# A gated-experts layer in fp32 on one core: the down projection as 2x4x4 block products in 26 multiplications (was 28), worked inside the unit that makes its inputs

## The chip, the core and the metric

The kernel runs on one core of one Trainium2 chip. The metric is the device time in microseconds of a whole execution, median of several runs. Beside the runs, one profiled execution is shown; its trace holds every instruction of every engine. The engines are named as the profile does: PE is TensorE (PEld its weight load), DVE is VectorE, ACT is ScalarE, POOL is GpSimd, SP is the engine whose queue issues most DMAs.

## The reference

The input x is (8, 512, 256): eight blocks of 512 tokens with 256 features. Its gates are (8, 8) and the shared gate is (8). There are eight experts and one shared expert, each with Wg and Wu (256 x 1024) and Wd (1024 x 256). All is fp32.

```python
g = jnp.einsum('bsd,edf->ebsf', h, Wg)
u = jnp.einsum('bsd,edf->ebsf', h, Wu)
expert_outs = jnp.einsum('ebsf,efd->ebsd', jax.nn.silu(g) * u, Wd)
expert_output = jnp.einsum('be,ebsd->bsd', gating_probs, expert_outs)
shared = jnp.einsum('bsf,fd->bsd', jax.nn.silu(h @ Sg) * (h @ Su), Sd)
out = x + (1.0 - sg) * expert_output + sg * shared
```

## The kernel before

**Tiling.** The batch is worked in two halves of four blocks (NH = 2, NI = 4). Features of an expert are taken in groups of 4 x 128 (GRP = 2). A *unit* is one half, one expert (nine with the shared one) and one group: 2 x 9 x 2 = 36 units, each numbered u.n. In a unit, a 4 x 4 grid of results h[i, j] (feature tile i of 128, batch block j of 512 tokens) is made for gate (m = 0) and up (m = 1), and then multiplied down to two tiles of 128 output features for each block.

**Gate and up products.** The grid with inner size 2 (256 features of x in two halves) isn't computed plainly with 32 products for each m, but with 26, by a scheme of shared terms. Each i has a number CI (0, 1, -1, 2). A *hub* makes the four diagonal results: P products (raw weights, first half of x), Q products accumulated on the same PSUM bank. The six pairs (i, j) in PAIRS then take three products each: an R1 product of a difference of weights U with a difference of inputs V, and two R products. `gate_up` (L549 on) is a generator: each of its 52 steps issues one product (a G). A hub has 16 of them, each of the six *blocks* of a pair 6. The bank that a pair's R1 accumulates on is seeded by ScalarE from f (`seed`, L417), which is the difference of two P results; f is made by `make_f` (L383), from a bank by VectorE (three pairs) or from SBUF copies by GpSimd (the other three). After R1, VectorE writes D minus the bank to a second bank (L437); after the last R product, it adds D (L450). `finish` (L353) then takes silu on ScalarE for m = 0, and for m = 1 VectorE multiplies silu, gate coefficient and bank to h (L363). GpSimd makes all weight forms: `make_at`, `w_difference` (U), `w_sums` (W, L282 and L276/L279).

**Down products.** `down` (L467) does the 4 x 4 grid of h as a 2 x 2 arrangement (I for features, J for blocks) of 2 x 2 products in seven multiplications (x = 1 to 7): 2 x 2 x 7 = 28 products a unit. The sums of h that they need (`T_sums`, L455) and of Wd (`load_d`, s, L339 to L342) are made on GpSimd. Each of the 14 sums over all units lives in SBUF (acc); it is copied into a PSUM bank by ScalarE (L482), two products are accumulated on it (L491), and ScalarE copies it back (L506). Two banks, po0 and po1, alternate for that. The 28 products of a unit are issued one by one (a D) among the G of the *next* unit.

**Order.** PE and POOL run in the order that the program writes (`manual_schedule`, HAND); in the first unit ACT too. For DVE and ACT a planner sets the order at build time. The strings HUB and BLOCKS say how G and D alternate. At the unit that closes a half, the results are combined, transposed back (`turn_back`, L531), added to x and stored; the next half's x is loaded and transposed meanwhile (`turn_x`, L138), and its forms of x are made (`make_forms`, L168) and kept in DRAM scratch, from where later units load v and b. The last unit's 28 D follow all G.

Of the kernel before, what the change touches and what calls it, by code (L numbers as in the profile page):

```python
# [16 lines left out]
def kernel(  # L17
# [30 lines left out]

    nc = tc.nc
# [10 lines left out]
    FBANK = 3  # L60

    PLAIN = ()
# [8 lines left out]
    ppool = ctx.enter_context(tc.tile_pool(name="p", bufs=16))  # L71
    hapool = ctx.enter_context(tc.tile_pool(name="ha", bufs=10))
    hbpool = ctx.enter_context(tc.tile_pool(name="hb", bufs=13))
    tpool = ctx.enter_context(tc.tile_pool(name="t", bufs=6))
# [3 lines left out]
    dpool = ctx.enter_context(tc.tile_pool(name="d", bufs=3))  # L78
# [44 lines left out]
    po_next = [0]  # L123

    def new_po(name, turns=False):

        k = po_next[0]
        if not turns:
            po_next[0] = 1 - k
        return ps_o.tile([P, S], F32, tag=f"po{k}", name=name), k  # L130
# [38 lines left out]
    def make_forms(h, p):  # L169

        i, j = PAIRS[p]
        d = CI[i] - CI[j]
        v, b0, b1 = (
            zpool.tile([P, S], F32, tag="z", name=f"f{k}{h}_{p}") for k in range(3)
        )
        ve.tensor_sub(v, xhub[h, i][:, 0], xhub[h, j][:, 0])
        if d != 1.0:
            nc.scalar.mul(v, v, 1.0 / d)
        ve.tensor_add(b0, v, xhub[h, j][:, 1])
        gp.tensor_tensor(b1, v, xhub[h, i][:, 1], ALU.add)  # L180
        made.append((h, p, (v, b0, b1)))
# [8 lines left out]
    def x_difference(u, p):  # L190

        i, j = PAIRS[p]
        if plain(u, p):
            return
        v = vpool.tile([P, S], F32, tag="v", name=f"v{u.name}_{p}")
        if (u.h, p) not in scratch:
            d = CI[i] - CI[j]
            ve.tensor_sub(v, xhub[u.h, i][:, 0], xhub[u.h, j][:, 0])
            if d != 1.0:
                nc.scalar.mul(v, v, 1.0 / d)  # L200
# [4 lines left out]
    def x_sums(u, p):  # L205
# [3 lines left out]
        if plain(u, p):  # L209
            return  # L210
# [37 lines left out]
    for h in range(NH):  # L248
        for e in range(NE):
            for g in range(GRP):  # L250
# [7 lines left out]
                u.wd, u.T, u.sg, u.store = {}, {}, {}, []  # L258
# [13 lines left out]
    def scaled_sum(out_, s, a, b, sub):  # L272

        if s in (1.0, -1.0):
            if s == 1.0:
                gp.tensor_tensor(out_, a, b, ALU.subtract if sub else ALU.add)  # L276
            else:
                assert not sub
                gp.tensor_tensor(out_, b, a, ALU.subtract)  # L279
        else:  # L280
            nc.scalar.mul(out_, a, s)  # L281
            gp.tensor_tensor(out_, out_, b, ALU.subtract if sub else ALU.add)  # L282

    def make_at(u, i):
# [5 lines left out]
        if CI[i] == 2.0 and (u.opens or units[u.n - 1].opens):  # L290
            gp.tensor_tensor(t, raw[:, :, 0], raw[:, :, 1], ALU.add)
            gp.tensor_tensor(t, t, raw[:, :, 0], ALU.add)
            u.at[i] = t
            return
        scaled_sum(t, CI[i], raw[:, :, 0], raw[:, :, 1], False)
        u.at[i] = t

    def plain(u, p):
        return u.n == 0 and p in PLAIN

    def w_difference(u, p):
        i, j = PAIRS[p]
        if plain(u, p):
            return
# [4 lines left out]
    def w_sums(u, p):  # L309
        i, j = PAIRS[p]  # L310
        d = CI[i] - CI[j]
        if plain(u, p):

            u.W[p] = []
            for r, (k, c) in enumerate(((i, CI[j]), (j, CI[i]))):
                a, A = u.raw[k][:, :, 0], u.raw[k][:, :, 1]
                if c != 0.0:
                    t = upool.tile([P, 2, P], F32, tag="u", name=f"m{u.name}_{p}_{r}")
                    scaled_sum(t, c, a, A, False)
                    A = t  # L320
                u.W[p].append(A)
            return
        W = bpool.tile([P, 2, 2, P], F32, tag="wb", name=f"wb{u.name}_{p}")
        scaled_sum(W[:, 0], -d, u.raw[i][:, :, 0], u.U[p], False)
        scaled_sum(W[:, 1], d, u.raw[j][:, :, 0], u.U[p], True)
        u.W[p] = W

    def load_d(u, pairs):
        for I in pairs:
            t = dpool.tile([P, 2, D], F32, tag="wd", name=f"wd{u.name}_{I}")  # L330
            r0 = (NI * u.g + 2 * I) * P
            nc.sync.dma_start(
                t,
                weights(u.e)[2][r0 : r0 + 2 * P].rearrange("(c p) d -> p c d", p=P),
            )
            s = dpool.tile([P, 4, P], F32, tag="sd", name=f"sd{u.name}_{I}")
            a11, a21 = t[:, 0, 0:P], t[:, 0, P : 2 * P]
            a12, a22 = t[:, 1, 0:P], t[:, 1, P : 2 * P]
            gp.tensor_tensor(s[:, 0], a21, a22, ALU.add)  # L339
            gp.tensor_tensor(s[:, 1], s[:, 0], a11, ALU.subtract)  # L340
            gp.tensor_tensor(s[:, 2], a11, a21, ALU.subtract)
            gp.tensor_tensor(s[:, 3], a12, s[:, 1], ALU.subtract)  # L342
            u.wd[I] = {
                1: a11, 2: a12, 3: s[:, 3], 4: a22, 5: s[:, 0], 6: s[:, 1], 7: s[:, 2]
            }

    def new_bank(u, m, name, spare=False):

        if spare and u.n == 0:
            turned[m] = False  # L350
            return ps_o.tile([P, S], F32, tag=f"po{m}", name=f"{name}{m}_{u.name}")
        return ps_g.tile([P, S], F32, tag=f"g{m}", name=f"{name}{m}_{u.name}")

    def finish(u, m, i, j, bank):
# [4 lines left out]
        else:  # L359
            b = NI * u.h + j  # L360
            pool, tag = (hapool, "ha") if j < 2 else (hbpool, "hb")
            t = pool.tile([P, S], F32, tag=tag, name=f"h{i}{j}_{u.name}")
# [6 lines left out]
    def P_step(u, i, m):  # L369
        bank = new_bank(u, m, f"c{i}{i}", i == 3)  # L370
# [4 lines left out]
        t = ppool.tile([P, S], F32, tag="p", name=f"P{i}{m}_{u.name}")  # L375
        nc.scalar.copy(t, bank)  # L376
        u.Ps[i, m] = t
        for p in range(FBANK):
            if max(PAIRS[p]) == i:
                make_f(u, p, m, bank)  # L380

    def make_f(u, p, m, bank=None):

        if plain(u, p) or (p, m) in u.f:
            return
        i, j = PAIRS[p]
        f = zpool.tile([P, S], F32, tag="z", name=f"f{i}{j}{m}_{u.name}")
        if bank is None:
            gp.tensor_tensor(f, u.Ps[j, m], u.Ps[i, m], ALU.subtract)  # L389
        elif i > j:  # L390
            ve.tensor_sub(f, u.Ps[j, m], bank)  # L391
        else:
            ve.tensor_sub(f, bank, u.Ps[i, m])
        u.f[p, m] = f

    def Q_step(u, i, m):
# [6 lines left out]
        t = ppool.tile([P, S], F32, tag="p", name=f"D{i}{m}_{u.name}")  # L403
        nc.scalar.copy(t, bank)  # L404
        u.Ds[i, m] = t

    def plain_step(u, p, m, r, k):
        i, j = PAIRS[p] if r == 0 else PAIRS[p][::-1]
        if k == 0:
            u.bank[i, j, m] = new_bank(u, m, f"c{i}{j}")  # L410
        nc.tensor.matmul(
            u.bank[i, j, m], u.W[p][r][:, m] if k else u.raw[i][:, m, 0],
            xhub[u.h, j][:, k], start=k == 0, stop=k == 1,
        )
        if k:
            finish(u, m, i, j, u.bank[i, j, m])

    def seed(u, p):

        i, j = PAIRS[p]  # L420
        for m in range(2 if not plain(u, p) else 0):
            u.bank[j, i, m] = new_bank(u, m, f"c{j}{i}", p % 2 == 1)
            nc.scalar.copy(u.bank[j, i, m], u.f[p, m])  # L423

    def R1_step(u, p, m):
        i, j = PAIRS[p]
        if plain(u, p):
            for k in range(2):
                plain_step(u, p, m, 0, k)
            return  # L430
# [8 lines left out]
    def R_step(u, p, m, r):  # L439
        if plain(u, p):  # L440
            plain_step(u, p, m, 1, r)
            return
# [11 lines left out]
    def T_sums(u, J, x):  # L454

        for I in range(2):
            h = {(r, c): u.h_.get((2 * I + r, 2 * J + c)) for r in range(2) for c in range(2)}
            a, b = {
                5: (h[0, 1], h[0, 0]), 6: (h[1, 1], u.T.get((J, I, 5))),
                7: (h[1, 1], h[0, 1]), 4: (h[1, 0], u.T.get((J, I, 6))),  # L460
            }[x]
            t = tpool.tile([P, S], F32, tag="t", name=f"T{x}_{I}{J}_{u.name}")
            eng = ve if I == 1 and u.n + 1 == len(units) else gp
            eng.tensor_tensor(t, a, b, ALU.subtract)  # L464
            u.T[J, I, x] = t

    def down(u, acc, last):  # L467


        for J in range(2):  # L470
            for n, x in enumerate((1, 5, 2, 6, 3, 7, 4) if last else (1, 5, 3, 2, 6, 7, 4)):
                ahead = (6, None, 7, 4)[n] if n < 4 else None
                if ahead:
                    T_sums(u, J, ahead)
                if n == 4 and J == 0:
                    T_sums(u, 1, 5)
                po, k = new_po(f"po{x}_{J}_{u.name}")
                opens = (J, x) not in acc
                seeded = not opens and not turned[k]
                turned[k] = False  # L480
                if seeded:
                    nc.scalar.copy(po, acc[J, x])  # L482
                for I in range(2):
                    b = {
                        1: u.h_[2 * I, 2 * J], 2: u.h_[2 * I + 1, 2 * J],
                        3: u.h_[2 * I + 1, 2 * J + 1],
                    }.get(x)
                    if b is None:
                        b = u.T[J, I, x]
                    first = not seeded and I == 0  # L490
                    nc.tensor.matmul(  # L491
# [60 lines left out]
    def gate_up(u, nxt):  # L552
# [34 lines left out]
        for p in range(len(PAIRS)):  # L587
# [12 lines left out]
            if p == 5:  # L600
                store_made()
# [147 lines left out]
```

## Time and profile before

| | before |
|---|---|
| median of three runs | 2524.13 us (2523.95 to 2524.53) |
| profiled execution, its own time | 2520.21 us |
| its span, first to last instruction | 2518.4 us |
| granted TensorE clock | 0.999 |
| HBM read, written | 227.84 MB, 13.63 MB |
| median time to landing of b, v, wd | 3.5, 2.6, 2.7 us |

The span lies within the execution's own time. A group of the profile gives the line, the engine and operation, output and inputs by their names in the program, the shapes and the count; then the busy time, the mean of one in ns, and how long the engine was idle just before instructions of this group, with what ended the idle time. Each 128x512 product leaves two records on PE, whose ends are modelled, so that records overlap; rates are best read from the starts. The rows by stage give, for a stretch of the span, its length and the busy time of each engine in it, with the number of instructions.

### The profile page before, as it was taken

To read this page: it belongs to the slowest core of one execution; us is meant where nothing else is said; L and a number is where in the kernel's file an instruction comes from. 1 tells how busy PE (TensorE), PEld (TensorE's weight loads), DVE (VectorE), ACT (ScalarE), POOL (GpSimd) and SP (SyncE) were. 2 spreads that over 40 slices of the span, in tenths; PEclk is the share of its full clock that TensorE was granted. 3 is DMA by queue.
4 is the path that set the end of the run, shared out by engine and by line. 5 is a ranking of instruction groups with operands and counts; after the bars stand their busy time and mean duration, and the time that the engine had idled before them with its cause. 6 is when DMAs were issued, how large, how long until landed. Compare 5 with 4: busy or idle time off the path is not lost.

```text
span 2518.4 us, 21862 instructions
## 1 busy us (share of the span) xinstructions
PE 2497.1 (99%) x5896; PEld 1107.9 (44%) x5896; DVE 1213.0 (48%) x1744; ACT 1493.3 (59%) x2798; POOL 1662.4 (66%) x1868
## 2 busy tenths in 40 slices
PE   8999999999999999999999999999999999999999
PEld 3444444444444444444444444444444444444444
DVE  6544444444444444444674444444444444444445
ACT  4566666656556666666444666666665656666663
POOL 6766666676666666666786666666676666666664
PEclk9999999999999999999999999999999999999999
DMA  4323233333323323322434322232233332332222
GB/s 168 100 84 91 89 89 89 94 101 96 97 89 99 88 84 92 88 91 87 162 129 123 99 89 80 88 96 88 87 98 97 100 97 88 100 88 80 89 84 83
DMA packets 181034, 242.92 MB, mean 96 GB/s; under 512 B 13872, under 2 KB 122416, under 8 KB 180912
## 3 DMA queue, kind: packets, MB, share of 16 engines
q1 hardware_dynamic: 180624, 241.49, 31.7%
q8 instruction: 48, 0.79, 0.1%
q14 instruction: 74, 0.61, 0.1%
q10 hardware_dynamic: 288, 0.04, 0.0%
HBM read 227.84 MB, written 13.63 MB: 96 GB/s over the span
## 4 chain that ended last, share of the span: by engine, by line
PE 98%; DMA 1%; DVE 0%; ACT 0%; issue 0%; SPq 0%; DVEq 0%; ACTq 0%
PE po L491 34%; PE c L445 29%; PE c L432 15%; PE c L398 10%; PE c L372 10%; DMA xin<-in_x_dram 1%; PE ptx L134 0%; PE pto L134 0%; DVE h L363 0%; ACT c L423 0%; DVE acc L508 0%; ACT to L543 0%; ACT wb L281 0%; DVE x L160 0%; DVE acc L512 0%
## 5 line engine op out<-in xcount | busy, mean ns | idle before, releaser
L445 PE MATMUL c<-b,wb 128*128 128x512 f32 x1728 | 815.4, 593 | 0.0
L363 DVE SCALAR_TENSOR_TENSOR h<-sg,coef,c 128x512 f32<-128x512 f32 x576 | 430.3, 747 | 609.5 <-PE c L445 374.7
L506 ACT COPY acc<-po 128x512 f32<-128x512 f32 x477 | 278.3, 583 | 447.0 <-PE po L491 442.4
L445 PEld LDWEIGHTS c<-b,wb 128*128 128x128 f32 x1728 | 328.2, 190 | 409.7 <-issue 383.7
L357 ACT ACTIVATE sg<-c 128x512 f32<-128x512 f32 x576 | 343.7, 597 | 216.1 <-PE c L445 118.6
L464 POOL TENSOR_TENSOR T<-h,h 128x512 f32<-128x512 f32 x284 | 357.3, 1274 | 145.7 <-PE po L491 98.0
L437 DVE TENSOR_TENSOR c<-D,c 128x512 f32<-128x512 f32 x432 | 299.7, 694 | 307.9 <-ACT sg L357 283.4
L282 POOL TENSOR_TENSOR wb<-wb,u 128x256 f32<-128x256 f32 x216 | 154.8, 738 | 443.5 <-ACT wb L281 443.5
L432 PE MATMUL c<-v,u 128*128 128x512 f32 x864 | 436.2, 593 | 8.2 <-ACT c L423 8.2
L491 PE MATMUL po<-T,sd 128*128 128x512 f32 x864 | 435.4, 593 | 1.9 <-ACT to L543 1.5
L450 DVE TENSOR_TENSOR c<-c,D 128x512 f32<-128x512 f32 x432 | 300.2, 695 | 213.4 <-PE c L445 212.8
L464 POOL TENSOR_TENSOR T<-h,T 128x512 f32<-128x512 f32 x284 | 356.7, 1278 | 13.1 <-PE po L491 13.1
L423 ACT COPY c<-f 128x512 f32<-128x512 f32 x432 | 255.7, 592 | 150.1 <-DVE h L363 114.7
L491 PE MATMUL po<-h,wd 128*128 128x512 f32 x576 | 293.5, 592 | 0.0
L482 ACT COPY po<-acc 128x512 f32<-128x512 f32 x465 | 276.3, 594 | 22.8 <-DVE acc L508 13.0
L372 PE MATMUL c<-x,w 128*128 128x512 f32 x576 | 276.3, 592 | 0.3 <-DVE x L158 0.3
L389 POOL TENSOR_TENSOR f<-P,P 128x512 f32<-128x512 f32 x216 | 272.6, 1277 | 0.0
L432 PEld LDWEIGHTS c<-v,u 128*128 128x128 f32 x864 | 164.0, 190 | 217.2 <-issue 180.5
L491 PEld LDWEIGHTS po<-T,sd 128*128 128x128 f32 x864 | 163.5, 190 | 206.4 <-issue 202.9
L398 PE MATMUL c<-x,at 128*128 128x512 f32 x432 | 203.0, 592 | 0.5 <-DVE f L391 0.5
L404 ACT COPY D<-c 128x512 f32<-128x512 f32 x288 | 168.0, 583 | 51.4 <-DVE h L363 51.3
L376 ACT COPY P<-c 128x512 f32<-128x512 f32 x288 | 165.1, 589 | 29.4 <-PE c L372 25.1
(67 smaller groups left out, 1722.2 us busy)
## 6 DMA issues: line engine op xcount, KB each, us to landing
b<-xs SPq DMA_DIRECT2D x207, 512.0 KB, 3.5
v<-xs SPq DMA_DIRECT2D x207, 256.0 KB, 2.6
w<-in_L_cond_Wg_dram SPq DMA_DIRECT2D x128, 128.0 KB, 3.3
w<-in_L_cond_Wu_dram SPq DMA_DIRECT2D x128, 128.0 KB, 3.3
wd<-in_L_cond_Wd_dram SPq DMA_DIRECT2D x64, 256.0 KB, 2.7
xs<-b SPq DMA_DIRECT2D x9, 512.0 KB, 2.9
xin<-in_x_dram SPq DMA_DIRECT2D x16, 256.0 KB, 4.3
xr<-in_x_dram SPq DMA_DIRECT2D x16, 256.0 KB, 3.1
```

Of the source, the lines that this page charges most:

```text
L357: nc.scalar.activation(s, bank, AF.Silu)
L363: ve.scalar_tensor_tensor(t, u.sg[i, j], coef[:, u.e, b : b + 1], bank, ALU.mult, ALU.mult)
L372: nc.tensor.matmul(bank, u.raw[i][:, m, 0], xhub[u.h, i][:, 0], start=True, stop=True)
L398: nc.tensor.matmul(bank, u.at[i][:, m], xhub[u.h, i][:, 1], start=False, stop=True, skip_group_check=True,)
L432: nc.tensor.matmul(bank, u.U[p][:, m], u.V[p], start=False, stop=True, skip_group_check=True)
L437: ve.tensor_sub(other, u.Ds[j, m], bank)
L445: nc.tensor.matmul(bank, u.W[p][:, r, m], u.VB[p][:, r], start=False, stop=True, skip_group_check=True,)
L450: ve.tensor_add(bank, bank, u.Ds[j, m])
L464: eng.tensor_tensor(t, a, b, ALU.subtract)
L482: nc.scalar.copy(po, acc[J, x])
L491: nc.tensor.matmul(po, u.wd[I][x], b, start=first, stop=True, skip_group_check=not first,)
L506: nc.scalar.copy(acc[J, x], po)
```

## The change

The down projection of a unit is now one scheme over the 4 x 4 grid, of the same family as the gate and up products: two output tiles, four feature tiles and four blocks in 26 products. For each pair (i, j) there are three: Wd form times h[i, j], Wd form times h[j, i], and the difference Ud times X = h[j, i] - h[i, j], accumulated on the first one's bank, which is held meanwhile. Eight more take, for each i, the sum of row i of h (p) and of column i of h (q). Down products of pair p are issued in the block after the one that makes its h, so they belong to the same unit; pair 5, p and q fall into the next unit's hub and first block (TAKE = 22). Rows and columns are summed by GpSimd (`add_sum`). Twenty sums over units are kept (b and B for the four i, S and V for the six pairs; `put` and `carried`); S and b travel through the bank by ScalarE copies, B and V are added by VectorE. At the end of a half `combos` bring them together, two of them behind each D (all at once in the last unit).

Further edits: all f are made by VectorE from the bank, and P of i = 3 isn't copied any more; h has one pool of 11 tiles; scalings of v go from ScalarE to VectorE; `make_at` uses GpSimd alone; Wd comes in one DMA, loaded a block before the unit begins; turned-back blocks are added by VectorE straight from PSUM; the order strings are regular (GGD), R1 and Q3 steps alternate in the hub; the first unit has 15 D of its own.

```diff
-    FBANK = 3
+    OWN = (0, 1, 2, 3, 4, 5)
...
     def new_po(name, turns=False):
         k = po_next[0]
+        if held[k]:
+            k = 1 - k
...
-            nc.scalar.mul(v, v, 1.0 / d)
+            ve.tensor_scalar(v, v, 1.0 / d, None, ALU.mult)
...
+    def at_of(t, c, a, A):
+        if c == -1.0:
+            gp.tensor_tensor(t, A, a, ALU.subtract)
+        else:
+            gp.tensor_tensor(t, a, A, ALU.add)
+            if c == 2.0:
+                gp.tensor_tensor(t, t, a, ALU.add)
...
-            gp.tensor_tensor(s[:, 0], a21, a22, ALU.add)
-            gp.tensor_tensor(s[:, 1], s[:, 0], a11, ALU.subtract)
-            gp.tensor_tensor(s[:, 2], a11, a21, ALU.subtract)
-            gp.tensor_tensor(s[:, 3], a12, s[:, 1], ALU.subtract)
+    def load_d(u):
+        t = dpool.tile([P, NI, D], F32, tag="wd", name=f"wd{u.name}")
+        r0 = NI * u.g * P
+        nc.sync.dma_start(
+            t, weights(u.e)[2][r0 : r0 + NI * P].rearrange("(c p) d -> p c d", p=P)
+        )
+        u.raw_d = t
+
+    def make_ad(u):
+        a, A = u.raw_d[:, :, 0:P], u.raw_d[:, :, P : 2 * P]
...
+                at_of(u.ad[i], CI[i], a[:, i], A[:, i])
+        u.a2 = dpool.tile([P, NI, P], F32, tag="a2", name=f"a2{u.name}", bufs=1)
+        nc.scalar.mul(u.a2, a, 2.0)
+
+    def d_forms(u, p):
+        i, j = PAIRS[p]
+        lo, hi = min(i, j), max(i, j)
+        U = upool.tile([P, P], F32, tag="ud", name=f"ud{u.name}_{p}", bufs=6)
+        gp.tensor_tensor(U, u.ad[i], u.ad[j], ALU.subtract)
+        W = upool.tile([P, 2, P], F32, tag="wd", name=f"wd{u.name}_{p}", bufs=6)
+        at, d = U.unsqueeze(1).to_broadcast([P, 2, P]), CI[i] - CI[j]
+        for c, a in ((2.0, u.a2), (1.0, u.raw_d)):
+            if d >= c:
+                gp.tensor_tensor(W, at, a[:, lo : hi + 1 : hi - lo, 0:P], ALU.subtract)
+                at, d = W, d - c
+        u.Ud[p] = U
+        u.Wd[p] = {lo: W[:, 0], hi: W[:, 1]}
...
-        for p in range(FBANK):
-            if max(PAIRS[p]) == i:
-                make_f(u, p, m, bank)
+        for p, (k, j) in enumerate(PAIRS):
+            if max(k, j) == i:
+                o = u.Ps[min(k, j), m]
+                t = o
+                if i < 3:
+                    t = zpool.tile([P, S], F32, tag="z", name=f"f{k}{j}{m}_{u.name}")
+                if k == i:
+                    ve.tensor_sub(t, o, bank)
+                else:
+                    ve.tensor_sub(t, bank, o)
...
+    def h_sums(u, p):
+        i, j = PAIRS[p]
+        u.X[p] = tpool.tile([P, S], F32, tag="t", name=f"X{p}_{u.name}")
+        ve.tensor_sub(u.X[p], u.h_[j, i], u.h_[i, j])
+        for k, l in ((i, j), (j, i)):
+            for which, n in (("rows", k), ("cols", l)):
+                u.sums.append((which, n, (k, l)))
+
+    def add_sum(u):
+        which, n, at = u.sums.pop(0)
...
+        gp.tensor_tensor(sums[n], u.h_[n, n] if first else sums[n], u.h_[at], ALU.add)
...
+        def put(key, bank, s):
+            if key not in acc:
...
+            elif s == 1.0:
+                ve.tensor_add(acc[key], bank, acc[key])
...
+        def carried(key, w, b):
+            po, k = new_po(f"{key[0]}{key[1]}_{u.name}")
+            seeded = key in acc and not turned[k]
+            turned[k] = False
+            if seeded:
+                nc.scalar.copy(po, acc[key])
+            nc.tensor.matmul(
+                po, w, b, start=not seeded, stop=True, skip_group_check=seeded
+            )
+            if seeded:
+                nc.scalar.copy(acc[key], po)
+            else:
+                put(key, po, 1.0)
...
+        def pair(p):
+            i, j = PAIRS[p]
+            d = CI[i] - CI[j]
+            A, k = single(("r", p), u.Wd[p][i], u.h_[i, j])
+            put(("B", j), A, 1.0)
+            held[k] = True
+            yield
+            if p in OWN:
+                carried(("S", p), u.Wd[p][j], u.h_[j, i])
...
+            yield
+            nc.tensor.matmul(
+                A, u.Ud[p], u.X[p], start=False, stop=True, skip_group_check=True
+            )
+            put(("V", p), A, 1.0)
+            held[k] = False
+            po_next[0] = 1 - k
+            if u.closes:
+                V, b = acc["V", p], (acc["b", i], acc["b", j])
+                if p in OWN:
+                    combos.append((V, -1.0, acc["S", p]))
+                    combos.append((acc["B", i], -1.0, acc["S", p]))
+                combos.append((b[0], 1.0 / d, V))
+                combos.append((b[1], -1.0 / d, V))
+            yield
...
+        for p in range(5):
+            yield from pair(p)
+        for what in ("p0", "q0", 5, "q1", "p1", "q2", "p2", "q3", "p3"):
+            if what == 5:
+                yield from pair(5)
+                continue
+            i = int(what[1])
+            if what[0] == "p":
+                flush_sums(u, "rows", i)
+                carried(("b", i), u.raw_d[:, i, 0:P], u.rows[i])
+            else:
+                flush_sums(u, "cols", i)
+                po, _ = single(("q", i), u.ad[i], u.cols[i])
+                put(("B", i), po, 1.0)
+            if u.closes and what in ("q0", "p1", "p2", "p3"):
+                ends_of(i)
+            yield
...
+        for what in "Q00 Q01 P10 P11 P20 P21 Q10 Q11 Q20 Q21 P30 P31 R00 Q30 R01 Q31".split()
...
+            if step == 2 and u.n:
+                make_ad(u)
+            if step in (3, 5, 7, 9, 11, 13) and u.n:
+                d_forms(u, (step - 3) // 2)
...
+        if u.n == 0:
+            make_ad(u)
+            for p in range(len(PAIRS)):
+                d_forms(u, p)
...
-    HUB = "GGDGGDGGGGDGGGGDGGDDGGDD"
-    BLOCKS = ("GDGGDGGGD", "GDGGDGGGD", "GDGGDGDGGD", "GDGGDGGGD", "GDGGDGGGD", "GDGGDGDGGD")
-    ORDER = HUB + "".join(BLOCKS)
-    FIRST = "DGGDGGDGG" + "G" * 46
+    HUB = "GGD" * 8
+    BLOCK = "GGDGGDGGD"
+    ORDER = HUB + BLOCK * 6
+    FIRST = "TGGTGGTGG" + "G" * 16 + BLOCK * 5
+    TAKE = 22
...
+                if nG > TAKE and nG % 2 == 0 and len(u.sums) > 0:
+                    add_sum(u)
+                if nG < TAKE and u.n and units[u.n - 1].sums:
+                    add_sum(units[u.n - 1])
...
+                next(behind, None)
                 since_close += 1
+                for _ in range(2 if nxt is not None else len(combos)):
+                    if combos:
+                        combine()
+                if since_close in BACK_AT:
+                    turn_back(u.h - 1, *BACK[BACK_AT.index(since_close)])
```

## The prediction

> **What bounds the kernel now.** I read the page's first lines, its groups, the busy time by stage, TensorE's waits, and the order of time in single stages. The page first:
>
> ```profile
> span 2518.4 us, 21862 instructions
> PE 2497.1 (99%) x5896; PEld 1107.9 (44%) x5896; DVE 1213.0 (48%) x1744; ACT 1493.3 (59%) x2798; POOL 1662.4 (66%) x1868
> ```
>
> TensorE is the bound. Every product of 128x512 leaves two records, so 5896 records are 2880 products (5760), 128 transposes and 8 opening ones. TensorE in order of time, in an ordinary unit:
>
> ```profile
> 1054.07 1.02 PE L432 MATMUL c<-v,u 128*128 128x512 f32 x2
> 1054.93 1.88 PE L445 MATMUL c<-b,wb 128*128 128x512 f32 x4
> ...
> 1071.24 1.02 PE L445 MATMUL c<-b,wb 128*128 128x512 f32 x2
> ```
>
> Between the first and the last start lie 20 products without a gap: 17.17 / 20 = 0.858 us each, whatever the mean of a record says. 2880 x 0.858 = 2471, the 128 transposes at 0.107 (four take 0.43) 14: so 2518 - 2485 = 33 us are lost somewhere. Busy time by stage (span of the stage; then PE, PEld, DVE, ACT, POOL):
>
> ```profile
> 0.00:71.40 71.40, 59.73 (x153) 25.96 (x154) 45.28 (x63) 33.31 (x63) 46.10 (x65) 0.98 0.51 168
> 1066.00:1134.00 68.00, 68.00 (x160) 30.13 (x159) 31.20 (x46) 41.43 (x79) 44.61 (x51) 1.00 0.30 92
> 1172.00:1240.00 68.00, 65.79 (x175) 29.67 (x174) 40.77 (x57) 34.12 (x64) 44.94 (x44) 1.00 0.45 147
> 1240.00:1309.00 69.00, 68.33 (x172) 31.02 (x171) 48.24 (x65) 36.59 (x68) 57.05 (x58) 1.00 0.36 118
> 2480.00:2518.00 38.00, 33.26 (x100) 15.30 (x98) 25.24 (x36) 11.64 (x20) 11.73 (x11) 1.00 0.21 63
> ```
>
> An ordinary unit (second row) loses nothing. The loss is in the first unit (start 7 us, then 52 products in some 61 us, about 16 over), at the change of halves (some 5), and in the last stage (2 of stalls, 4 for the last add and store). Notice the fourth row: VectorE at 70%, GpSimd at 83%, and TensorE still loses only 0.7 us. The groups that the change replaces or loads:
>
> ```profile
> L363 DVE SCALAR_TENSOR_TENSOR h<-sg,coef,c 128x512 f32<-128x512 f32 x576 | 430.3, 747 | 609.5 <-PE c L445 374.7
> L506 ACT COPY acc<-po 128x512 f32<-128x512 f32 x477 | 278.3, 583 | 447.0 <-PE po L491 442.4
> L464 POOL TENSOR_TENSOR T<-h,h 128x512 f32<-128x512 f32 x284 | 357.3, 1274 | 145.7 <-PE po L491 98.0
> L437 DVE TENSOR_TENSOR c<-D,c 128x512 f32<-128x512 f32 x432 | 299.7, 694 | 307.9 <-ACT sg L357 283.4
> L389 POOL TENSOR_TENSOR f<-P,P 128x512 f32<-128x512 f32 x216 | 272.6, 1277 | 0.0
> ```
>
> VectorE in order of time, where it is crowded:
>
> ```profile
> 1281.80 1.76 DVE L512 TENSOR_TENSOR acc<-acc,acc 128x512 f32<-128x512 f32 x1
> 1283.48 0.68 DVE L437 TENSOR_TENSOR c<-D,c 128x512 f32<-128x512 f32 x1
> 1284.08 0.69 DVE L450 TENSOR_TENSOR c<-c,D 128x512 f32<-128x512 f32 x1
> 1284.68 0.68 DVE L502 TENSOR_TENSOR acc<-po,acc 128x512 f32<-128x512 f32 x1
> 1285.39 1.76 DVE L504 TENSOR_TENSOR acc<-acc,acc 128x512 f32<-128x512 f32 x1
> ```
>
> Back to back, an add with a PSUM operand costs 0.60 us (1284.08 to 1284.68), not 0.69; h costs 0.7; an add of two SBUF tiles 0.6 to 1.7 (the 20 of L176, L179, L198, L214, L504, L510 and L512 in 1206 to 1322 average 1.17). GpSimd the same way: 1.22 for 128x512, 0.69 for 128x256, 0.44 for 128x128.
>
> [...] 1.76 above against a steady 0.69 for L450; GpSimd's L464 took 1.72 instead of 1.27 twice near the end. [...]
>
> **The change, part by part.** A unit is one group of 512 features of one expert for half the batch: 36 units.
>
> TensorE: 28 down products become 3 x 6 + 8 = 26. 2 x 36 x 0.858 = 61.8 us less. This is sure, as those products stand on the path that sets the end.
>
> VectorE, per ordinary unit, before 31.6: f, all 12 now from banks, not 6 (+6 x 0.60); six differences X of two SBUF tiles (+6 x 1.17); 16 adds of down results into SBUF sums, formerly ScalarE copies (+16 x 0.60). 31.6 + 3.6 + 7.0 + 9.6 = 51.8 of a unit of 78 x 0.858 = 66.9: 77%. In a block (6 gate-up and 3 down products, 7.72 us): 6 PSUM adds 3.6, two h 1.4, X 1.2: 6.2, so 1.5 is free. In the hub (16 + 8 products, 20.6 us): 12 f, 2 subtractions, 5 down adds 11.4, four h 2.8, X 1.2: 15.4. It fits. Where f of P3 is read from the bank just before Q30, six reads (3.6 us) lie between P30's end at 13.7 us of the hub and Q31 at 18.9, three between it and Q30 at 16.3: 0.5 us of slack. This costs nothing as long as VectorE is not behind by then; otherwise 0.5 us a unit.
>
> ScalarE: loses some 26 copies of acc and po, two P and one scaling; gains 20 copies and one 128x512 scaling. Lighter; nothing on the path.
>
> GpSimd, before 45: loses 16 T and 6 f (22 x 1.22 = 26.8) and 8 sd (3.5); gains 24 row and column sums (29.3), 4 ad, 6 Ud (10 x 0.44), 7 Wd (4.8), one at (0.7). 45 - 30.3 + 39.2 = 54: 81%. No row shows a broadcast operand (Wd): between 0.69 and, as an estimate, twice that, 0 to 4.8 us a unit; I take 0.69, for the runs inside it are as long as L282's halves. Stage by stage: hub and block 0 hold 30 us of it in 28.3, blocks 1 to 5 4 to 6 each in 7.72. So the hub is where it lags. After the last product of the unit before releases the wb buffer stand 5 weight forms (3.5), 7 sums (8.5), ad (1.7) and three d_forms (3.4) ahead of q2's column sum: 17.1 us, and q2 is the 24th product, 23 x 0.858 = 19.7. Slack 2.6. q1 needs c1 after 10, and starts at 14.6. Both hold.
>
> PSUM: the two down banks alternate, and a pair holds one over three down products (7.7 us); a carried sum needs the bank drained (0.6), seeded (0.6) and two hops of 0.2, within the 5.1 us between two uses. Hidden in the units. Without gate-up products beside it (tail) it isn't: a bank then turns in 0.86 + 1.6 us for two products, 1.23 each instead of 0.86.
>
> DMA: one wd load instead of two, a block ahead; SP's queue gets shorter. Nothing.
>
> **What the closing stages give back.** Unit 17 and the last one also combine: four VectorE operations on two SBUF tiles for each pair, 3 at the ends: 27 x about 1.0 (0.6 to 1.7).
> - Unit 17, blocks 2 to 5: 4 x 6.2, 16 combos 16, next half's forms 7, turns 2: 50 us against 31 + 2. As TensorE slows, GpSimd thins out and the costs fall, and some 3 us of lead is used up: 10 us lost. Unit 18's hub with nine combos and the turned-back adds: 34 of VectorE in 29.6: 5. Together 15, before 5: +10.
> - Last unit: the same combos, no forms: +5.
> - Tail: 11 down products at 1.23 (+4), then the turns, no longer interleaved, behind the last combo (+2): +6.
> - First unit: f no longer waits for GpSimd, and 15 down products fill stalls; but ad and d_forms (9 us of GpSimd) stand ahead of block 0's forms: -2, between -10 and +8.
> - Ordinary units: 34 small unknowns, +3.
>
> Sum: 2518.4 - 61.8 + 10 + 5 + 6 - 2 + 3 = 2478.6 of span. The profiled execution took 2520.2, 1.8 beside its span, and the median of runs is 3.9 above that: 2484.
>
> **Rivals.**
> - *Full gain* (0.13): combos fall into idle slots or stay last in VectorE's order, and the first unit gains: 2524 - 62 + 6 (tail) = 2468. For it: row 1240 to 1309. Against: the 50 us above.
> - *GpSimd late in the hub* (0.15): each of the 7 sums takes 1.72 instead of 1.22, or Wd is dear: 17.1 + 3.5 = 20.6 against 19.7, 0.9 us a unit, x 34 = 30: 2514. Still faster. Against: only six X per unit contend.
> - *VectorE becomes the bound, slower* (0.15): at the head of its queue a subtraction waits some 2 us for ScalarE's silu in each block (L437; 1.99 at 1068.63) while adds of down results, ready, stand behind. 6.2 + 2.0 = 8.2 against 7.72: 0.5 us in each of 5 x 36 blocks, 90 us: 2574. It decides from 0.25 us a block on (45 us over 180 blocks eat what is left of the gain). Against: with the natural order the wait is filled by the last block's h, X and add, and row 1240 to 1309 had it all at 70%.
> - *No difference* (0.05): a mixture around 2524. That the change doesn't do what it says is excluded by the count: 26 products come out of the loops.
>
> **How the numbers follow.** Likeliest (0.52): 2484, its own range 2470 to 2500. Faster by over 0.2% (5 us, about what a measurement of this kernel can tell from no change): 0.52 + 0.13 + 0.15 = 0.80; within it 0.05; slower 0.15. The range 2462 to 2525 leaves out the slower case and a little below the full gain.
>
> **What would show it.** Right: 5752 TensorE records; an ordinary unit of 66.9 us with no wait; VectorE near 75% and GpSimd near 81%; waits of TensorE bunched in the first unit, 17 and 18 and the last, on VectorE. Wrong: an ordinary unit above 67.5 us: with TensorE waiting for GpSimd's rows or cols, the second rival; for VectorE's c or po, the third.

## The result and the profile after

The changed kernel takes 2514.34 us (median of five runs, 2513.45 to 2516.66) against 2524.13 before: a ratio of 0.9964, interval 0.9949 to 0.9979. It is faster, as forecast, but by 10 us where 40 were forecast. The profiled execution is 2516.66 us with a span of 2514.8, so the spans compare as 2518.4 to 2514.8, 3.6 us less; that execution was the slowest of the five.

The head of the page of the changed kernel, engine by engine:

```profile
span 2514.8 us, 22640 instructions
PE 2454.0 (98%) x5752; PEld 1079.7 (43%) x5752; DVE 1891.1 (75%) x2758; ACT 1328.8 (53%) x2484; POOL 2080.4 (83%) x2296
```

The 144 records (72 products) of the forecast are gone, and VectorE and GpSimd stand at 75% and 83% (77% and 81% were worked out). Busy time by stage (length; then PE, PEld, DVE, ACT, POOL, the granted TensorE clock, DMA), in four stages: the first unit, an ordinary unit, the unit that closes a half, and the last unit with the tail:

```profile
0.00:77.00 77.00, 62.79 (x155) 26.76 (x156) 48.70 (x70) 33.56 (x63) 54.25 (x74) 0.96 0.44 147
1541.00:1608.00 67.00, 67.00 (x157) 29.55 (x156) 50.40 (x75) 36.89 (x70) 56.85 (x64) 1.00 0.31 95
1207.00:1295.00 88.00, 71.29 (x168) 30.87 (x169) 84.15 (x111) 32.98 (x60) 63.95 (x60) 0.93 0.40 125
2405.50:2514.80 109.30, 83.84 (x207) 36.09 (x205) 88.38 (x119) 40.91 (x75) 67.02 (x66) 0.95 0.22 65
```

An ordinary unit is what the sum said: 67.0 us, TensorE without a gap, VectorE at 75%. The loss is in the closing stages, where VectorE is busy for 84 of 88 us and TensorE for 71. VectorE's groups that answer to those shown of before, and the new ones on two SBUF tiles:

```profile
L361 DVE SCALAR_TENSOR_TENSOR h<-sg,coef,c 128x512 f32<-128x512 f32 x576 | 428.5, 744 | 359.7 <-PE c L421 248.0 <-PE c L392 55.2 <-POOL rows L446 41.0
L416 DVE TENSOR_TENSOR c<-D,c 128x512 f32<-128x512 f32 x432 | 299.4, 693 | 91.0 <-ACT sg L356 69.6 <-PE c L411 12.4
L435 DVE TENSOR_TENSOR X<-h,h 128x512 f32<-128x512 f32 x216 | 212.8, 985 | 5.9
L557 DVE TENSOR_TENSOR accV<-accV,accS 128x512 f32<-128x512 f32 x12 | 16.1, 1344 | 0.0
L557 DVE TENSOR_TENSOR accB<-accB,accS 128x512 f32<-128x512 f32 x12 | 14.2, 1179 | 2.8 <-ACT accS L487 2.8
L557 DVE TENSOR_TENSOR accb<-accb,accV 128x512 f32<-128x512 f32 x12 | 12.7, 1097 | 0.0
L559 DVE SCALAR_TENSOR_TENSOR accb<-accV,accb 128x512 f32<-128x512 f32 x12 | 11.8, 1016 | 0.0
```

The wait for ScalarE's silu ahead of L416 fell from 283 to 70 us: the third rival's mechanism didn't arise. The combining operations (L557, L559; two smaller groups add 4.5 us) took 59.3 us for 54, 1.10 each.

TensorE's loss by stage, in all runs below, is worked out from its order of time: the time from the first Q product of a unit to that of the next, less 0.858 us a product and 0.107 a transpose. With the last store's distance from TensorE's end, the differences make up the 3.6 us:

| us of span | forecast | before | after | difference |
|---|---|---|---|---|
| 72 products at 0.858 | -61.8 | | | -61.8 |
| units 17 and 18 | +10 | 3.6 + 1.0 | 18.5 + 9.3 | +23.2 |
| last unit, tail, end | +5 and +6 | 2.0 + 4.3 | 24.4 + 6.9 | +25.0 |
| first unit | -2 | 12.8 | 17.4 | +4.6 |
| 32 ordinary units | +3 | 3.3 | 8.7 | +5.4 |
| sum | -39.8 | | | -3.6 |

### The profile page after: what moved, and what is told of

It reads as the page before. It is cut to its first block, busy times and chain, and to the rows that moved or that the text cites. A ratio compares the mean times of both kernels' runs of the same rounds, so it can differ in the third digit from the quotient of the medians.

```text
span 2514.8 us, 22640 instructions
## 1 busy us (share of the span) xinstructions
PE 2454.0 (98%) x5752; PEld 1079.7 (43%) x5752; DVE 1891.1 (75%) x2758; ACT 1328.8 (53%) x2484; POOL 2080.4 (83%) x2296
## 4 chain that ended last, share of the span: by engine, by line
PE 93%; DVE 4%; issue 1%; ACT 1%; DMA 0%; POOL 0%; DVEq 0%; SPq 0%; ACTq 0%; POOLq 0%
PE c L421 28%; PE c L411 14%; PE c L392 10%; PE c L370 10%; PE r L511 7%; PE S L483 7%; PE r L494 7%; PE b L483 5%; PE q L494 5%; DVE h L361 1%; DVE accV L557 1%; DVE X L435 0%; DVE c L426 0%; DVE accB L557 0%; DVE accb L557 0%
## 5 line engine op out<-in xcount | busy, mean ns | idle before, releaser
L411 PE MATMUL c<-v,u 128*128 128x512 f32 x864 | 445.0, 597 | 16.4 <-ACT c L406 11.5
L446 POOL TENSOR_TENSOR rows<-rows,h 128x512 f32<-128x512 f32 x288 | 383.8, 1333 | 3.8 <-DVE h L361 3.8
L446 POOL TENSOR_TENSOR cols<-cols,h 128x512 f32<-128x512 f32 x288 | 369.6, 1283 | 0.0
L416 DVE TENSOR_TENSOR c<-D,c 128x512 f32<-128x512 f32 x432 | 299.4, 693 | 91.0 <-ACT sg L356 69.6
L312 POOL TENSOR_TENSOR wb<-u,wb 128x256 f32<-128x256 f32 x108 | 80.9, 749 | 295.4 <-ACT wb L310 295.4
L426 DVE TENSOR_TENSOR c<-c,D 128x512 f32<-128x512 f32 x432 | 299.2, 693 | 22.8 <-PE c L421 21.3
L511 PE MATMUL r<-X,ud 128*128 128x512 f32 x432 | 224.0, 600 | 11.2 <-DVE accB L470 11.2
L483 PE MATMUL S<-h,wd 128*128 128x512 f32 x432 | 222.1, 596 | 6.5 <-ACT S L482 6.4
L494 PE MATMUL r<-h,wd 128*128 128x512 f32 x432 | 221.5, 594 | 0.0
L435 DVE TENSOR_TENSOR X<-h,h 128x512 f32<-128x512 f32 x216 | 212.8, 985 | 5.9
L446 POOL TENSOR_TENSOR rows<-h,h 128x512 f32<-128x512 f32 x144 | 207.2, 1439 | 0.0
L482 ACT COPY S<-accS 128x512 f32<-128x512 f32 x201 | 119.0, 592 | 140.1 <-DVE accV L470 132.1
L446 POOL TENSOR_TENSOR cols<-h,h 128x512 f32<-128x512 f32 x144 | 186.7, 1296 | 0.0
```

What stands on the lines that cost most here:

```text
L411: nc.tensor.matmul(bank, u.U[p][:, m], u.V[p], start=False, stop=True, skip_group_check=True)
L416: ve.tensor_sub(other, u.Ds[j, m], bank)
L426: ve.tensor_add(bank, bank, u.Ds[j, m])
L446: gp.tensor_tensor(sums[n], u.h_[n, n] if first else sums[n], u.h_[at], ALU.add)
L483: nc.tensor.matmul(po, w, b, start=not seeded, stop=True, skip_group_check=seeded)
L494: nc.tensor.matmul(po, w, b, start=True, stop=True)
```

## The experiments

Theory Q: VectorE's queue is full at the close of a half, and the combining operations in it are what TensorE pays for. Rival B: the blocks turned in and back, the two alternating banks and a lower clock after stalls cost it. TensorE's waits in the changed kernel speak against a third one, GpSimd: from 1172 to 1310 us none of them is for GpSimd, and from 2440 us on 1.8 of some 19 us are. GpSimd enters at most through VectorE.

**Without the combining operations.**

```diff
-        elif s in (1.0, -1.0):
-            ve.tensor_tensor(to, to, what, ALU.add if s > 0 else ALU.subtract)
-        else:
-            ve.scalar_tensor_tensor(to, what, s, to, ALU.mult, ALU.add)
```

> Leaves out the arithmetic of all 27 combining operations of each half (the sums V, B and b are stored uncombined); everything else as in the changed kernel. Theory Q (VectorE's queue: the combining operations stand in it ahead of the adds and differences that TensorE needs, and fill it at the close of a half): of the 53 us that TensorE wastes in the two closing stages (28 from 1172 to 1306, 24 from 2445 to the end), some 30 go: about 2484 us. Rival B (the turned-in and turned-back blocks, the two alternating banks and the lower clock after a stall cost it, not the combining): at most 8 us go, 2506 or more.

2475.78 us, ratio 0.9809 (0.9795 to 0.9824). The 54 operations cost 38.5 us. The losses of units 17 and 18 fall to 2.6 and 3.5, that of the last unit and tail to 4.2. By stage, the blocks of the closing half and those of the last unit:

```profile
1206.00:1242.00 36.00, 34.40 (x89) 15.24 (x88) 32.59 (x46) 15.88 (x30) 32.50 (x30) 1.00 0.59 190
2412.00:2452.00 40.00, 39.93 (x94) 17.32 (x92) 32.12 (x48) 18.35 (x36) 31.66 (x29) 1.00 0.26 78
```

The same place in the changed kernel:

```profile
1209.00:1247.50 38.50, 28.63 (x64) 11.89 (x62) 37.87 (x45) 9.99 (x18) 26.82 (x21) 0.91 0.59 183
2449.00:2489.00 40.00, 26.70 (x58) 10.44 (x58) 40.00 (x49) 11.56 (x21) 30.23 (x23) 1.00 0.09 26
```

At 91% and 80% of VectorE TensorE loses 1.6 of 36 us and nothing; at 98% and 100% it issues 64 and 58 records instead of some 90. Of rival B, the turned blocks and the two banks are still in this run, and they don't cost the time by themselves. The lower clock isn't: it went with the stalls (granted clock 0.998 here, 0.994 in the changed kernel), so it is a part of the price. So is the wait of the turned-back blocks for their combined sums, which this run doesn't have either.

**S straight from its bank**, in the closing units, where the bank was not just turned.

```diff
-            if p in OWN:
+            own = p in OWN
+            if own and u.closes and not turned[po_next[0] if not held[po_next[0]] else 1 - po_next[0]]:
+                own = False
+                o, _ = new_po(f"S{p}_{u.name}")
+                nc.scalar.copy(o, acc["S", p])
+                nc.tensor.matmul(
+                    o, u.Wd[p][j], u.h_[j, i], start=False, stop=True, skip_group_check=True
+                )
+                put(("B", i), o, -1.0)
+                put(("V", p), o, -1.0)
+            elif own:
```

> In the closing units only, V and B take S straight from its PSUM bank (two adds with one SBUF operand at 0.60 us) instead of by a ScalarE copy and two operations on two SBUF tiles (1.2 us each as measured); where the bank was just used for a transpose, the old way stays. Theory Q: VectorE saves about 12 x 2 x 0.6 = 14 us in each half less what stays, TensorE some two thirds of it: about 2500 us. Rival B: no change, 2510 to 2516.

2510.49 us (0.9946; 0.9931 to 0.9961): 4 us less, not 14. Eighteen of 24 operations fell to 0.67 us, but the 24 on b rose from 1.06 to 1.26: VectorE's combining time went from 59.3 only to 54.2 us. The amount was misjudged: the expectation counted 24 operations on S in each half, and there are 24 in both together.

**b on its bank as well**, in the closing units: the V terms wait in lists, and go onto the bank after b's last product.

```diff
-                combos.append((b[0], 1.0 / d, V))
-                combos.append((b[1], -1.0 / d, V))
+                vs.setdefault(i, []).append((1.0 / d, V))
+                vs.setdefault(j, []).append((-1.0 / d, V))
...
+            for n, (s, V) in enumerate(vs[i]):
+                to = acc[key] if n + 1 == len(vs[i]) else po
+                ve.scalar_tensor_tensor(to, V, s, po, ALU.mult, ALU.add)
```

> As the run before, and in the closing units the 12 additions of V into b are made on the PSUM bank that holds b's last product (0.60 us each, one SBUF operand, no GpSimd in the way), so that they leave the blocks and go to the four p steps. Theory Q: the blocks 2 to 5 lose 4.6 us of VectorE each, and the p steps bear 1.8 each: about 2490 us. Rival B: the banks are held longer, so not better than the run before, or worse by up to 8 us.

2501.12 us (0.9904; 0.9889 to 0.9919), short of 2490. All 24 take 0.68 us now, one SBUF operand each; combining time is 40.5 us. Unit 17 loses 7.9, but unit 18, where the p steps are, 13.8. The four kernels lie on a line:

| | VectorE on combining, us | time, us |
|---|---|---|
| changed kernel | 59.3 | 2514.3 |
| S from the bank | 54.2 | 2510.5 |
| b too | 40.5 | 2501.1 |
| left out | 0 | 2475.8 |

0.6 to 0.75 us of time go with each us of VectorE. The least, 0.62, is that of the last step, and no kernel lies between 0 and 40 us, so a lead of a few us that absorbs the beginning isn't excluded; a large one is.

**The tail on six banks.** The last 11 down products take the free gate and up banks in turn.

> The changed kernel, but the last 11 down products, which have no gate and up products beside them, go to the six free gate and up banks in turn instead of the two down banks. If bank turns set the tail (my 1.23 us a product): 5 to 8 us less, about 2508. If the tail waits for VectorE's queue behind the combining operations (theory Q): at most 3 us less, 2511 or more.

2513.87 us: no change (last stage 22.8 instead of 24.4). My price of 1.23 us for a product in the tail didn't bind. What bound it stands in VectorE's order of time in the changed kernel. The bank that pair 5's S needs is free when q's result has been added into B, and that add comes behind the combining of pair 4:

```profile
2484.75 1.41 DVE L557 TENSOR_TENSOR accV<-accV,accS 128x512 f32<-128x512 f32 x1
2486.08 1.74 DVE L435 TENSOR_TENSOR X<-h,h 128x512 f32<-128x512 f32 x1
2487.75 1.74 DVE L557 TENSOR_TENSOR accB<-accB,accS 128x512 f32<-128x512 f32 x1
2489.41 1.28 DVE L557 TENSOR_TENSOR accb<-accb,accV 128x512 f32<-128x512 f32 x2
2490.62 0.68 DVE L470 TENSOR_TENSOR accB<-q,accB 128x512 f32<-128x512 f32 x1
```

and TensorE, which waits through it:

```profile
2485.19 1.02 PE L494 MATMUL r<-h,wd 128*128 128x512 f32 x2
2491.97 2.07 PE L483 MATMUL S<-h,wd 128*128 128x512 f32 x2 [5.76 <-ACT S L482]
2493.84 1.92 PE L511 MATMUL r<-X,ud 128*128 128x512 f32 x2
```

With six banks S no longer waits, but the product on X does, for the add of r into B that comes behind the same operations:

```profile
2490.07 1.02 PE L487 MATMUL S<-h,wd 128*128 128x512 f32 x2
2495.03 2.04 PE L515 MATMUL r<-X,ud 128*128 128x512 f32 x2 [3.94 <-DVE accB L474]
```

**Place or amount.** Two kernels leave the combining as it is and move it in the blocks. The first was meant to put all four operations of a pair behind the next block's add into B. Its condition does something else: `nd % 3 == 2` holds at a block's third down product, not at its second. So in unit 17 all four stand at once ahead of that add, where the changed kernel has two of them. In the last unit all four stood there before, and nothing changes.

```diff
-                for _ in range(2 if nxt is not None else len(combos)):
+                for _ in range((4 if nd % 3 == 2 else 0) if in_blocks else 2 if nxt is not None else len(combos)):
```

> The same combining operations, but within the blocks of the closing units all four of a pair are issued behind the second down product of the next block (after that block's add into B, which frees the held bank), not two behind the third and two behind the next first. If their place ahead of the add into B is what costs (head of the queue): 10 us less or more, about 2503. If the sum of VectorE's work in these blocks is what counts (theory Q): within 4 us of 2514.

2522.13 us (ratio 1.0; 0.9992 to 1.0009): 8 us more than the changed kernel, and no test of the expectation, as the operations went the other way. VectorE in unit 17:

```profile
1215.81 1.75 DVE L557 TENSOR_TENSOR accV<-accV,accS 128x512 f32<-128x512 f32 x1
1217.48 1.21 DVE L557 TENSOR_TENSOR accB<-accB,accS 128x512 f32<-128x512 f32 x1
1218.61 3.42 DVE L557 TENSOR_TENSOR accb<-accb,accV 128x512 f32<-128x512 f32 x2
...
1222.55 0.68 DVE L470 TENSOR_TENSOR accB<-r,accB 128x512 f32<-128x512 f32 x1
```

Units 17 and 18 lose 22.7 and 14.2 us here, against 18.5 and 9.3; the last unit, which is as it was, 23.2 against 24.4. The operations also took 64.3 us in all instead of 59.3, so the amount rose with the change of place. Further ahead of the add is worse; a kernel with all of them behind it wasn't run. The second kernel issues them singly behind four of six gate and up products.

```diff
+                if final and nG > TAKE and nG % 3 != 0 and combos:
+                    combine()
...
-                for _ in range(2 if nxt is not None else len(combos)):
+                for _ in range(0 if final and nG > TAKE else 2):
```

> The changed kernel with the same combining operations in the blocks of the closing units, issued singly behind four of a block's six gate and up products, not two behind a down product (and four at once in the fifth run, which cost 8 us more). If bursts in VectorE's queue are the price (each holds up the next result that TensorE waits for): 8 us less or more, about 2505. If it is the amount of VectorE's work, or of its waits for GpSimd: within 4 us of 2514.

2514.15 us (0.9964; 0.9950 to 0.9977): no change. Spreading them is worth nothing beside pairs. Yet the operations took only 52.9 us in this order; by the line above some 4 us should have gone, about as much as the interval can tell. So VectorE's time alone doesn't set TensorE's: the place matters too, and how the 38.5 us divide between place and amount stays open.

**The same load on the kernel before.** First with inputs that are always there:

```diff
+                        ve.tensor_add(load_t, xhub[u.h, 0][:, 0], xhub[u.h, 1][:, 1])
```

> The kernel before, with some 25 additions of two SBUF tiles (128x512, their result unused) put into VectorE's queue over the blocks of each closing unit and the hub after it, where the changed kernel has its combining operations. Theory Q (the same operations cost little where VectorE is busy for 48%): at most 6 us more, 2524 to 2530. If such operations cost TensorE time by themselves (by holding up GpSimd): 15 us or more, 2539 and above.

2540.25 us (1.0071; 1.0054 to 1.0088), which says little on the closing stages: the planner had brought the first of the 52 operations forward to 12.9 us, and the losses grew in unit 0 (12.8 to 20.7) and in units 19 to 34 (2.7 to 10.1). Then with inputs made just before:

```diff
+                        ve.tensor_add(load_t, acc[0, (1, 5)[n]], newest[-1])
```

> The kernel before with 52 additions of two SBUF tiles of 128x512, results unused, in VectorE's queue at the two closing stages; their inputs are a tile of h just made and a running sum, so that the planner can't bring them forward (in the seventh run it had, into the first units of each half). Theory Q: where VectorE has half its time free, the same work costs TensorE less than a quarter of the 0.65 us per us of the changed kernel: under 10 us, 2524 to 2533. If such operations cost time by themselves: 25 us or more.

2546.40 us (1.0089; 1.0074 to 1.0103): 22 us more for 57.4 us of VectorE, 0.39 each. That is more than theory Q allowed. The group, and the stages:

```profile
L696 DVE TENSOR_TENSOR load<-acc,h 128x512 f32<-128x512 f32 x52 | 57.4, 1103 | 0.8
```

```profile
1209.00:1247.50 38.50, 31.71 (x80) 14.14 (x79) 37.53 (x46) 11.66 (x22) 31.16 (x26) 0.94 0.56 177
2466.00:2492.00 26.00, 22.96 (x54) 9.75 (x53) 24.04 (x26) 12.81 (x25) 21.26 (x19) 1.00 0.33 95
```

VectorE's average of 48% is no spare at this place: the closing half has the forms of x on it, and with the load it is 97% busy there. In the last unit it is 92%, and TensorE stands still for 3 of these 26 us. So the load costs in the kernel before too, at some 60% of the price, and 22 us lie nearer to the 25 of operations that cost time by themselves than to theory Q's 10. Theory Q holds as far as the combining in VectorE's queue is what TensorE pays for; that such work is nearly free wherever VectorE's average is low doesn't hold.

**Order in the first unit.** ScalarE's order there left to the planner.

```diff
-        tc.manual_schedule(engines=HAND | {mybir.EngineType.Activation})
+        tc.manual_schedule(engines=HAND)
```

> The changed kernel, with ScalarE's order in the first unit left to the planner like in all others. If the first unit's waits for ScalarE's seeds (11 us in six places) come from the order by hand, with copies of S now in it: 4 to 8 us less, about 2508. If they come from forms of x and of weights being late: no change, 2512 to 2516.

2518.69 us (0.9985; 0.9978 to 0.9992): not faster. The first unit's loss was 16.8 us here and 15.1 to 17.4 in the unchanged kernel, but it isn't the same loss. The waits for seeds fell from 11.5 to 1.1 us, and a single one took their place. TensorE, and ScalarE ahead of it:

```profile
35.00 3.78 PE L370 MATMUL c<-x,w 128*128 128x512 f32 x4 [9.67 <-ACT D L398]
33.35 0.63 ACT L333 ACTIVATE a<-wd 128x512 f32<-128x512 f32 x1 [11.07 <-POOL wd L345]
```

The planner put a scaling of Wd (L333) ahead of the copies of D, and there it waits for GpSimd's down forms. The same scaling waits 3.54 us in the unchanged kernel. So the planner's order is no better than that by hand; that a third would be isn't excluded.

**A better version.** The kernel with S and b on banks, the tail on six banks, and the last half's blocks turned back as their sums are ready. A first form seeded banks on which transposes had just run, and its sums are not the right ones:

> The third run's kernel (S and b combined on PSUM banks in the closing units), the last 11 down products on the six free banks, and the last half's turned-back blocks issued as their sums are ready, not after all products. Theory Q with bank turns now binding in the tail (2.5 us waits for ScalarE's seeds in the third run): 8 us less than the third run, about 2493. If the tail only waits for VectorE: about 2499.

It took 2496.79 us. The second form turns back on the two down banks:

```diff
+        if tail:
+            tail.append(1)
+            return ps_g.tile([P, S], F32, tag=f"g{len(tail) % 2}", name=name), 0
...
-            pt = ps_g.tile([P, S], F32, tag=f"g{r}", name=f"pto{b}_{r}")
+            pt = ps_o.tile([P, S], F32, tag=f"po{r}", name=f"pto{b}_{r}")
...
     for _ in behind:
+        for at in due:
+            turn_back(*at)
         while combos:
             combine()
+        due = list(ends)
```

> The third run's kernel (S and b combined on PSUM banks), with the last 11 down products on six free banks and the last half's blocks turned back on the two down banks as soon as their sums are ready. If the tail is bound by bank turns after the blocks' overload is eased (2.5 us waits for ScalarE's seeds, three times): 5 to 8 us less than the third run, about 2495. If it only waits for VectorE: 2500.

2496.02 us, 0.9892 of before (0.9877 to 0.9908): faster than both kernels. Against the kernel with b on its bank, the end behind TensorE's last instruction shrank from 6.2 to 4.1 us, the last stage only from 14.4 to 13.2. The changed kernel, run again beside it:

> The changed kernel unchanged, on the same chip as the others of this call: 2514 us, 0.996 of before.

2515.35 us, 0.9972 (0.9961 to 0.9982).

## Why the prediction was right or wrong

**Right.** The 61.8 us of products, the ordinary unit (67.0 us; VectorE 50.4 for 51.8 worked out, GpSimd 56.8 for 54), the hub on GpSimd without a wait that counts, and the places of the losses. Of the rivals, GpSimd late in the hub and VectorE's head-of-queue wait in ordinary blocks did not come (the Wd forms with a broadcast operand, L345, took 0.73 us each). That the former had 2514 us, the time measured, is chance: from 90 to 1170 us no wait of TensorE is for GpSimd.

**Wrong: the step "What the closing stages give back", by its size.** It had the mechanism and the demand: 50 us of VectorE against 33 in unit 17's blocks. It then wrote part of the deficit off: "As TensorE slows, GpSimd thins out and the costs fall, and some 3 us of lead is used up: 10 us lost", and +5 for the last unit. The runs show nothing written off: unit 17 alone lost 18.5 us, against a deficit of 17. Costs did not fall: X took 1.18 on average from 1170 to 1345 us and 1.22 in the last stage, against 0.97 before 1170. The link to GpSimd is in the traces: of the 36 adds of two SBUF tiles at L176 to L214 and L504 to L512 of the kernel before, the seven with GpSimd idle beside them took 0.68 to 0.69 us, and the 21 with GpSimd busy throughout 1.28 on average, while those with a PSUM operand (L437, L450, L502, L508) took 0.69 either way; in the changed kernel those of L435 and L557 took 0.68 (14) and 1.07 (199). GpSimd did thin out, from 56.85 of 67.0 us in an ordinary unit to 26.82 of 38.5 in unit 17's blocks, and X cost more all the same. A lead of 3 us isn't excluded, but it would be a small part. Measured, the two closings and the tail grew by 48.2 us, not 21. Terms, as far as they can be told apart: 12 us written off (17 to 10, and 5 for the last unit, where 17 less 7 for the forms is 10); 5 for operations at 1.10 instead of 1.0; some 8.7 for products at half clock (below), which the prediction has no term for. This division is argued from the trace; that the combining operations carry 38.5 us is shown.

**Wrong in a term: the tail.** +6 for bank turns and late turns. The trace of the kernel before has 0.58 us for the copy out (L506), 0.59 for the seed (L482), 0.20 from the end of a product of 0.858 to the copy (1068.66 to 1069.72) and 0.14 from a seed to TensorE (2500.53 to 2500.67): 1.51 us for a turn priced at 1.6. Six banks alone gave nothing, six banks and early turns together about 3 us on the span of the better version. What TensorE waited for there stood in VectorE's queue behind the combining.

**Wrong in sign: the first unit**, -2 forecast, +4.6 measured; in the second profile of the same kernel +2.3, and 1.4 more ahead of the first Q product. Its waits for ScalarE's seeds are 11.5 us, against 8.2 before, and it has two stretches at half clock of 3.4 us each (from 26.05 and 43.12), not one (from 32.94). The down forms on GpSimd hold up ScalarE (3.5 us at L333); how much of the loss that is, and whether the forms of x on VectorE come late, wasn't tried and stays open.

**Row 1240 to 1309 of the kernel before** was read as proof that 70% of VectorE and 83% of GpSimd cost nothing. In the run without combining, 91% went with 1.6 of 36 us lost; in the kernel before with the load, 92% went with 3 of 26. It said nothing on 98%.

## What to carry to other kernels

Where an engine is asked for more than a stage holds, count the whole deficit as lost, unless a run shows a lead (17 us counted, 18.5 lost in unit 17); an average over the kernel, and a rate at 70%, don't speak for a stage at 100%. Work done once per half is cheap in the sum over a kernel (here 59 us of VectorE in 1891) and dear at its place (38 us of time). Reading one operand from the PSUM bank that has just been written, and not from SBUF, took the operations from 1.1 to 1.3 us down to 0.68, and was worth 13 us here, with no instruction less to do.

## What the runs showed of the hardware that was not expected

Behind some of its waits, TensorE comes back at half its clock. In the changed kernel, the stages behind waits of 4.0, 1.9, 5.8 and last 3.4 us (the number behind POOL's bracket is the granted clock):

```profile
1222.00:1226.50 4.50, 4.36 (x9) 2.30 (x10) 3.87 (x7) 1.43 (x4) 1.10 (x1) 0.50 0.51 119
1292.40:1295.80 3.40, 3.40 (x5) 1.35 (x4) 2.31 (x4) 0.84 (x2) 0.17 (x1) 0.50 0.27 83
2491.90:2497.20 5.30, 5.23 (x6) 1.80 (x6) 1.38 (x2) 1.19 (x3) 0.00 (x0) 0.50 0.00 0
2481.80:2485.60 3.80, 3.33 (x7) 1.32 (x8) 3.80 (x6) 1.19 (x2) 2.48 (x3) 1.00 0.00 0
```

The three products from 2491.97 took 5.3 us instead of 2.6. With the stage from 1248.0 to 1252.4, at 0.61, some 8.7 us were lost in the closing stages in this way, an estimate: half of the time that TensorE worked at half clock. The run without combining has a mean clock of 0.998, the changed kernel 0.994. At 1292.4 half clock lasted 3.4 us. It came behind waits as short as 2.3 us (25.96) and 1.9 us (1291.67), and not behind 2.4 us (1208.17) or 3.4 us (2481.77). So in this kernel the length of a single wait doesn't tell whether the clock falls.

The other is of the planner, not of the chip: in the kernel before with a load, an addition whose inputs had long been ready did not stay where the program wrote it. The planner moved it by more than 1100 us, into a stage that had no room.
